# The second norm's products on 64-row halves of TensorE's array, in a kernel of four residual layers

## The chip, the cores and the metric

The kernel runs on one core of a Trainium2 chip. The metric is the device time of one execution in microseconds (us). The engines have these names in the profile: PE (TensorE, the matrix engine, with PEld for its weight loads), DVE (VectorE), ACT (ScalarE), POOL (GpSimd) and SP (SyncE, which here issues transfers). A product of the program in 32-bit floats shows in the trace as two weight loads and two matmul instructions.

## The reference

The input is 8 images of 64 channels, 128 x 128 pixels, in 32-bit floats. Four layers are applied, each as `x = x + L(_gn(x))`, where `_gn` is a group norm over 32 groups. L0 is a deformable convolution, L1 a 3x3 convolution, L3 a neighbour graph with a convolution and an attention factor. The change is in L2:

```python
def _s5_block(x, i, ...):                    # x: (images, 16384 positions, 64 channels)
    fx = _layer_norm(x, ln1_g[i], ln1_b[i])  # first norm, over the channels
    h = _s5_scan(fx, ...)                    # complex state-space scan, forward and backward
    x = jax.nn.gelu(h) + fx
    fx2 = _layer_norm(x, ln2_g[i], ln2_b[i]) # second norm, over the channels
    return fx2 @ ff_enc[i].T @ ff_dec[i].T + fx2
y_h = _s5_block(<positions row by row>, 0, ...)
y_v = _s5_block(<positions column by column>, 1, ...)
return einsum(concat(y_h, y_v), fusion_w) + fusion_b
```

## The kernel before

The images go through in four pairs; a tile has 2 x 64 = 128 partitions. Layer 0 (gathers issued by POOL) takes about the first 12,110 us. After it each pair passes the first norm, and then layer 2 in class `Scan`: direction d = 0 takes the positions row by row, d = 1 column by column. For each pair and direction `ahead` makes 16 steps g, each of 8 rows (or columns); that is 4 x 2 x 16 = 128 steps. Four successive positions are numbered 2h + e: in the scan's tiles e is the half of the 128 partitions, h and the image i are free dimensions, and 256 blocks of four positions are the innermost.

One step of `ahead` (the state of the backward scan was written to memory before) does these things, with the names of the tiles:

- `inputs` (L1236-1246): ACT scales the normed input into `fx`, and SP issues four loads `in<-fx`, which bring the two images' channels and the position parities into their partitions.
- `drive` (L1248-1262): PE makes `pv` from `in`, ACT copies it to `v` (one buffer), PE turns it into `pt`, DVE multiplies both by cosines and sines into `u` and `v`, and POOL adds them: `u`.
- `scan` (L1264-1277): DVE runs the recurrence, two instructions, into `z`; PE makes the start state `pn`.
- `rebuilt` (L1294-1308): for the backward state, loaded by SP into `zb` (one buffer), and for `z`: PE turns it into `zt`, POOL multiplies into `x` (L1305), DVE makes `xt`, POOL subtracts (L1307).
- `outputs` (L1310-1325): per half h, PE adds four products into `py`, ACT applies gelu, DVE adds the input: `h`.
- `mixed` (L1327-1345): the second norm. Its weights are folded ahead of time into two 128 x 128 matrices side by side, `outs[:, CEN : MIX + P]`: the centring (times 1/8) and the centring times `(ff_enc, ff_dec, ln2_g, fusion)`. Both are block-diagonal, one 64 x 64 block for each e. Per half h there are four products (m: which 128 of the 256 blocks; i: which image) with a 128 x 128 piece of `h` as weights and the 256 columns as moving operand, into `pc`, one PSUM bank for each m. ACT squares the centred 128 columns of each product into `qs` (named `sq` in the code) and copies the mixed ones to `ms`; DVE sums the squares over the channels to `var` (L1343). The reciprocal root of the variances, `rsqrt` (L112-122, tiles `ln_ve`, `ln_sh`, `ln_y`, `ln_t`), is a chain of 15 small DVE operations.
- `add` (L1347-1362): POOL multiplies `ms` by `ln_y` (L1353, two instructions), PE transposes back (`tp`, L1357), DVE adds to the running sum `room` (L1359) and, in d = 1, takes statistics for the next group norm (L1362).

Beside the steps of d = 0 the backward scan of d = 1 runs (`back`, through the generator `aside`), which doubles the `drive` and `scan` work of these steps; beside the last steps of d = 1 the end of layer 0 for the next pair runs. The PSUM tiles have three tags with two banks each (`x` for `pc`, `y` for `py`, `b` for `pv`, `pt` and `zt`) and two banks for small ones. The program lists the operations in the order of the code; which instruction stands where in each engine's queue is decided when it is built, by a scheduler, and an engine then takes them in that order.

```python
for m in range(2):
    pc = net.ps.tile([P, 2, 2 * P], F32, tag="x", name=f"pc{tag}_{h}{m}")
    for i in range(2):
        nc.tensor.matmul(pc[:, i], lhsT=hs[:, h, i, m * P : (m + 1) * P], rhs=self.outs[:, CEN : MIX + P], start=True, stop=True)
```

Of the kernel before, what the change touches and what calls it, by code (L numbers as in the profile page):

```python
# [9 lines left out]
F32 = mybir.dt.float32  # L10
I32 = mybir.dt.int32
AF = mybir.ActivationFunctionType
# [4 lines left out]
P = 128  # L17
C = 64
# [18 lines left out]
OUTM, INM, CEN, MIX = 0, T * P, T * P + 3 * P, T * P + 4 * P  # L37
# [1178 lines left out]
class Scan:  # L1216
# [110 lines left out]
    def mixed(self, g, hs):  # L1327

        nc, net, tag = self.nc, self.net, f"{self.p}_{self.d}_{g}"
        ms = [self.wp.tile([P, 2, 4, C], F32, tag=f"ms{h}", name=f"ms{tag}_{h}") for h in range(2)]
        var = net.small.tile([P, 16], F32, tag="var", name=f"var{tag}")
        for h in range(2):
            sq = self.wp.tile([P, 4, P], F32, tag="sq", name=f"qs{tag}_{h}", bufs=1)
            for m in range(2):
                pc = net.ps.tile([P, 2, 2 * P], F32, tag="x", name=f"pc{tag}_{h}{m}")
                for i in range(2):
                    nc.tensor.matmul(pc[:, i], lhsT=hs[:, h, i, m * P : (m + 1) * P], rhs=self.outs[:, CEN : MIX + P], start=True, stop=True)  # L1339
                nc.scalar.activation(sq[:, 2 * m : 2 * m + 2], pc[:, :, 0:P], AF.Square)  # L1340
                to = ms[h][:, :, 2 * m : 2 * m + 2].rearrange("p e i c -> p i e c")
                nc.scalar.copy(to, pc[:, :, P:].rearrange("p i (e c) -> p i e c", e=2))
            nc.vector.tensor_reduce(var[:, 8 * h : 8 * h + 8], sq.rearrange("p q (e c) -> p (q e) c", c=C), axis=mybir.AxisListType.X, op=ALU.add)  # L1343
            yield
        yield ms, net.rsqrt(net.small, var, 16, EPS, "ln16")
# [18 lines left out]
    def ahead(self, aside):  # L1364


        self.outs = self.wp.tile([P, NOUT], F32, tag="outs", name=f"outs{self.p}_{self.d}", bufs=1)
        self.nc.sync.dma_start(self.outs, self.net.out_tab[self.d])
        fxs, us, xs, late, z = {}, {}, None, None, None
        for g in range(-2, NG + 1):  # L1370
            if 0 <= g + 1 < NG:
                z = self.scan(0, g + 1, us.pop(g + 1), z, "z")
            hs = self.outputs(g, fxs.pop(g), xs) if 0 <= g < NG else None
            mixed = self.mixed(g, hs) if 0 <= g < NG else None
            if 0 <= g + 1 < NG:
                xs = [self.rebuilt(1, g + 1, None)]
            if mixed:
                next(mixed)
            if 0 <= g + 1 < NG:
                xs.append(self.rebuilt(0, g + 1, z))  # L1380
            if g + 2 < NG:
                fxs[g + 2] = self.inputs(0, g + 2, "in", "fx")
                us[g + 2] = self.drive(0, g + 2, fxs[g + 2])
            made = None
            if mixed:
                next(mixed)
                made = (g, *next(mixed))
            if late:
                self.add(*late)
            late = made  # L1390
            next(aside, None)
        for _ in aside:
            pass
# [48 lines left out]
```

## Time and profile before

| | |
|---|---|
| median of 10 runs | 16340.71 us (16333.48 to 16350.54) |
| profiled execution: its time, and its span from first to last instruction | 16354.39 us, 16352.6 us |
| mean granted clock of TensorE over the span | 0.823 |
| busy over the span: PE, DVE, POOL, ACT | 66%, 71%, 62%, 18% |
| layer 2's four stretches of 32 steps (first to last `py`) | 613.5, 611.4, 608.7, 596.4 us |
| a steady step of d = 0, of d = 1 | 21.4, 15.7 us |

The table's shares are means over stages with different limits: the gathers of layer 0 fill POOL for the first three quarters of the span, and say nothing of layer 2. So layer 2's own stretches are what to read. A step is counted from one group's first `py` to the next one's. In rows of the profile "idle before <-" names what ended the wait of an engine ahead of an instruction.

### The profile page before, as it was taken

To read this page: it belongs to the slowest core of one execution; us is meant where nothing else is said; L and a number is where in the kernel's file an instruction comes from. 1 tells how busy PE (TensorE), PEld (TensorE's weight loads), DVE (VectorE), ACT (ScalarE), POOL (GpSimd) and SP (SyncE) were. 2 spreads that over 40 slices of the span, in tenths; PEclk is the share of its full clock that TensorE was granted. 3 is DMA by queue.
4 is the path that set the end of the run, shared out by engine and by line. 5 is a ranking of instruction groups with operands and counts; after the bars stand their busy time and mean duration, and the time that the engine had idled before them with its cause. 6 is when DMAs were issued, how large, how long until landed. Compare 5 with 4: busy or idle time off the path is not lost. (4 is left out here: it accounts for less than half of the span.)

```text
span 16352.6 us, 119261 instructions
## 1 busy us (share of the span) xinstructions
PE 10871.1 (66%) x31736; PEld 4000.6 (24%) x31736; DVE 11662.1 (71%) x27948; ACT 2880.9 (18%) x4762; POOL 10194.1 (62%) x10484
## 2 busy tenths in 40 slices
PE   7864576367665635766556655643489888888896
PEld 2211121112211111211111111111135344344343
DVE  6777777777777777777777777777547558466566
ACT  1100111011000001110000000000144244243342
POOL 5777777777777777777777777777425135044142
PEclk9986798678887767988778877865699899999997
DMA  5444444345433334443333343333422433434223
GB/s 171 126 120 134 138 144 151 111 140 149 146 114 118 115 112 139 146 124 114 118 115 116 115 119 115 114 108 108 124 65 70 150 78 103 117 82 136 87 69 106
DMA packets 900135, 1933.41 MB, mean 118 GB/s; under 512 B 199932, under 2 KB 435844, under 8 KB 876420
## 3 DMA queue, kind: packets, MB, share of 16 engines
q0 software_dynamic: 442368, 1208.55, 25.5%
q1 hardware_dynamic: 382048, 679.50, 13.7%
q10 hardware_dynamic: 75044, 37.72, 1.1%
q8 instruction: 257, 4.21, 0.1%
q14 instruction: 418, 3.42, 0.1%
HBM read 1540.74 MB, written 208.10 MB: 107 GB/s over the span
## 5 line engine op out<-in xcount | busy, mean ns | idle before, releaser
L380 POOL DMA_INDIRECT g<-table,idx x9216 | 8721.2, 946 | 2823.9 <-issue 2631.9
L391 DVE TENSOR_TENSOR g<-g,corner_weights 128x256 f32<-128x256 f32 x9216 | 3768.7, 415 | 2722.6 <-DMA g<-table,idx 2685.4
L392 DVE TENSOR_REDUCE sm<-g 128x64 f32<-128x256 f32 x9216 | 5013.8, 579 | 8.9
L292 PE MATMUL po<-xe,wt 128*54 128x512 f32 (+3 forms) x8384 | 4300.9, 628 | 11.9 <-ACT ob L302 11.9
L398 PE MATMUL sp<-ident,sm 128*128 128x128 f32 x4096 | 1537.3, 380 | 4165.5 <-DVE sm L392 4151.1
L398 PEld LDWEIGHTS sp<-ident,sm 128*128 128x128 f32 x4096 | 630.2, 156 | 6732.4 <-DVE sm L392 5045.9
L403 ACT COPY s<-sp 128x512 f32<-128x512 f32 x1024 | 599.8, 586 | 8720.2 <-PE sp L398 8719.7
L292 PEld LDWEIGHTS po<-xe,wt 128*54 128x54 f32 x8384 | 902.8, 132 | 1343.0 <-issue 1062.4
L409 PE MATMUL yp<-s,wd 128*64 128x512 f32 (+1 forms) x2560 | 897.3, 711 | 25.6 <-ACT s L403 24.8
L891 POOL COPY l_yb<-ln_y 128x512 f32<-128x512 f32 x128 | 73.0, 615 | 1298.3 <-DVE ln_y L122 1298.3
L1261 POOL TENSOR_TENSOR u<-u,v 128x512 f32<-128x512 f32 x256 | 328.1, 1282 | 692.8 <-DVE v L1260 550.3
L607 PE MATMUL c<-room,l_w 128*64 128x508 f32 (+1 forms) x3072 | 741.8, 597 | 22.5 <-DMA room<-nx 14.0
L1353 POOL TENSOR_TENSOR ms<-ms,ln_y 128x512 f32<-128x512 f32 x256 | 274.2, 1092 | 638.8 <-DVE ln_y L122 608.4
L1243 ACT ACTIVATE fx<-room,ln_b,ln_g 128x512 f32<-128x512 f32 x512 | 639.1, 1292 | 172.4 <-DMA in<-fx 149.5
L1276 DVE TENSOR_TENSOR_SCAN z<-tabs,z,u 128x256 f32<-128x256 f32 x512 | 435.2, 876 | 214.7 <-POOL u L1261 186.0
L1254 PE MATMUL pv<-in,tabs 128*128 128x512 f32 x1024 | 509.2, 620 | 45.5 <-DVE u L1260 40.8
L1339 PE MATMUL pc<-outs,h 128*128 128x256 f32 x2048 | 501.8, 388 | 30.3 <-DVE h L1324 28.9
L1321 PE MATMUL py<-x,outs 128*128 128x512 f32 x1024 | 507.4, 599 | 7.8 <-POOL x L1307 7.3
L1321 PE MATMUL py<-in,outs 128*128 128x512 f32 x1024 | 505.6, 606 | 4.4 <-DMA outs<-out_tab 2.3
L1339 PEld LDWEIGHTS pc<-outs,h 128*128 128x128 f32 x2048 | 396.3, 195 | 207.4 <-issue 113.2
L1307 POOL TENSOR_TENSOR x<-x,xt 128x512 f32<-128x512 f32 x256 | 348.2, 1360 | 130.6 <-DVE xt L1306 130.1
L609 DVE TENSOR_TENSOR room<-room,c 128x512 f32<-128x512 f32 x128 | 87.9, 686 | 436.9 <-PE c L607 400.5
(416 smaller groups left out, 10175.8 us busy)
## 6 DMA issues: line engine op xcount, KB each, us to landing
g<-table,idx POOLq DMA_INDIRECT x9216, 2.7
in<-fx SPq DMA_DIRECT2D x1024, 128.0 KB
xe<-in_x_dram SPq DMA_DIRECT2D x56, 1408.0 KB
table<-q SPq DMA_DIRECT2D x256, 256.0 KB
y<-ys SPq DMA_DIRECT2D x128, 256.0 KB
room<-in_x_dram SPq DMA_DIRECT2D x64, 512.0 KB
yr<-y SPq DMA_DIRECT2D x64, 512.0 KB
room<-nx SPq DMA_DIRECT2D x256, 128.0 KB
```

The lines of the kernel that those rows point to most:

```text
L292: nc.tensor.matmul(po[:, r0:r1, c0:c1], lhsT=wt[:, t, :], rhs=xe[:, row + r0 : row + r1, c0 + dx : c1 + dx], start=n == 0, stop=n == len(u ...
L380: nc.gpsimd.indirect_dma_start(out=tq[:, k, :], out_offset=None, in_=flat[i], in_offset=bass.IndirectOffsetOnAxis(ap=idx[:, at : at + 1], ...
L391: nc.vector.tensor_mul(t[:, ks], t[:, ks], w)
L392: nc.vector.tensor_reduce(sm[:, ks], t[:, ks].rearrange("p k q c -> p k c q"), axis=mybir.AxisListType.X, op=ALU.add)
L398: nc.tensor.transpose(sp[:, j, :], sm[:, j * P : (j + 1) * P], self.ident)
L403: nc.scalar.copy(st[i][:, :, m * P : (m + 1) * P], sp)
L409: nc.tensor.matmul(yp[half[i], :], lhsT=wd[rows, j, :], rhs=src[rows, :], start=j == 0, stop=j == 4)
L607: nc.tensor.matmul(o, lhsT=lt, rhs=mv, start=k < 2, stop=k >= len(calls) - 2)
L1243: nc.scalar.activation(fx[:, e].rearrange("p h (o m) -> p h o m", m=self.INNER), src[:, e::2], AF.Identity, bias=w["ln1_b"], scale=w["ln1_g"])
L1254: nc.tensor.matmul(pv, lhsT=tabs[:, at : at + P], rhs=fx[:, :, h, :], start=h == 0, stop=h == 1)
L1321: nc.tensor.matmul(py, lhsT=lt, rhs=mv, start=n == 0, stop=n == len(calls) - 1)
L1339: nc.tensor.matmul(pc[:, i], lhsT=hs[:, h, i, m * P : (m + 1) * P], rhs=self.outs[:, CEN : MIX + P], start=True, stop=True)
```

## The change

`mixed` uses the block-diagonal form. Each product is made twice, once for each e: 64 partitions of `h` as weights, with the 64 rows of `outs` that belong to them, and of these the 64 + 64 columns of their own blocks (two strided runs). The two products of a pair go to different halves of the array's rows, and their results to two PSUM banks `pc[0]` and `pc[1]`, both of tag `x`; a bank now holds one e of all four (m, i), where it held both e of one m. In instructions of the trace, a step has 32 matmuls on 64 rows with 128 columns, where it had 16 on 128 rows with 256 columns. The number of ACT instructions and of their elements stays; a pair of them now waits for all products of its bank. The rest of the code is as it was, three lines further down; the built order of instructions on the engines differs in the steps of layer 2.

```diff
--- before.py
+++ after.py
@@ -1333,13 +1333,16 @@
         var = net.small.tile([P, 16], F32, tag="var", name=f"var{tag}")
         for h in range(2):
             sq = self.wp.tile([P, 4, P], F32, tag="sq", name=f"qs{tag}_{h}", bufs=1)
+            pc = [net.ps.tile([P, 4, 2, C], F32, tag="x", name=f"pc{tag}_{h}{e}") for e in range(2)]
             for m in range(2):
-                pc = net.ps.tile([P, 2, 2 * P], F32, tag="x", name=f"pc{tag}_{h}{m}")
                 for i in range(2):
-                    nc.tensor.matmul(pc[:, i], lhsT=hs[:, h, i, m * P : (m + 1) * P], rhs=self.outs[:, CEN : MIX + P], start=True, stop=True)
-                nc.scalar.activation(sq[:, 2 * m : 2 * m + 2], pc[:, :, 0:P], AF.Square)
-                to = ms[h][:, :, 2 * m : 2 * m + 2].rearrange("p e i c -> p i e c")
-                nc.scalar.copy(to, pc[:, :, P:].rearrange("p i (e c) -> p i e c", e=2))
+                    for e in range(2):
+                        rows = slice(e * C, (e + 1) * C)
+                        both = self.outs[rows, CEN : MIX + P].rearrange("p (k e c) -> p k e c", k=2, e=2)[:, :, e]
+                        nc.tensor.matmul(pc[e][:, 2 * m + i], lhsT=hs[rows, h, i, m * P : (m + 1) * P], rhs=both, start=True, stop=True)
+            for e in range(2):
+                nc.scalar.activation(sq[:, :, e * C : (e + 1) * C], pc[e][:, :, 0], AF.Square)
+                nc.scalar.copy(ms[h][:, e], pc[e][:, :, 1])
             nc.vector.tensor_reduce(var[:, 8 * h : 8 * h + 8], sq.rearrange("p q (e c) -> p (q e) c", c=C), axis=mybir.AxisListType.X, op=ALU.add)
             yield
         yield ms, net.rsqrt(net.small, var, 16, EPS, "ln16")
```

## The prediction

> **What bounds the kernel now.** I read the page first for the groups of the changed lines, then the windows view for two stretches of steady steps, then the timelines of PE, POOL, ACT and SP in one step of each kind. From the page (line, engine, operation, tiles, count, busy us and mean ns, idle time before them):
>
> ```profile
> L1261 POOL TENSOR_TENSOR u<-u,v 128x512 f32<-128x512 f32 x256 | 328.1, 1282 | 692.8 <-DVE v L1260 550.3
> L1353 POOL TENSOR_TENSOR ms<-ms,ln_y 128x512 f32<-128x512 f32 x256 | 274.2, 1092 | 638.8 <-DVE ln_y L122 608.4
> L1339 PE MATMUL pc<-outs,h 128*128 128x256 f32 x2048 | 501.8, 388 | 30.3 <-DVE h L1324 28.9
> L1339 PEld LDWEIGHTS pc<-outs,h 128*128 128x128 f32 x2048 | 396.3, 195 | 207.4 <-issue 113.2
> ```
>
> The changed products are 2048 instructions, 502 us of PE: 16 in each of 128 steps (four pairs, two directions, 16 groups). What a step is bound by differs by direction. The windows view, five steps along the rows, then six along the columns (length, then busy time of PE, PEld, DVE, ACT, POOL; clock):
>
> ```profile
> 12206.50:12313.50 107.00, 95.08 (x301) 50.77 (x300) 66.22 (x156) 49.67 (x91) 49.58 (x41) 1.00 0.30 74
> 12499.65:12593.85 94.20, 93.95 (x312) 53.58 (x311) 83.53 (x174) 41.48 (x84) 52.06 (x43) 1.00 0.21 52
> ```
>
> A row step takes 21.40 us, and PE is idle for 2.4 of them; a column step takes 15.70, and PE has no idle time. The clock is full in both, so the durations compare. PE in a column step (start, us, instruction, count):
>
> ```profile
> 12509.16 1.02 PE L1301 MATMUL zt<-zb,turn 128*128 128x512 f32 x2
> 12510.01 1.89 PE L1339 MATMUL pc<-outs,h 128*128 128x256 f32 x8
> 12511.74 1.02 PE L1301 MATMUL zt<-z,turn 128*128 128x512 f32 x2
> 12512.60 1.89 PE L1339 MATMUL pc<-outs,h 128*128 128x256 f32 x8
> 12514.33 0.60 PE L1357 MATMUL tp<-ident,ms 128*128 128x128 f32 x4
> 12514.76 0.28 PE L1269 MATMUL pn<-z,tabs 128*128 128x2 f32 x2
> ```
>
> From start to next start a block of eight takes 1.73 us, 0.216 a product of 256 columns; a product of 512 takes 0.43; four products of 128 take 0.43, 0.108 each with a full weight load each. In the row step PE's waits hang on other engines (its timeline, then ACT's and POOL's):
>
> ```profile
> 12217.88 1.98 PE L1254 MATMUL pv<-in,tabs 128*128 128x512 f32 x4 [0.89 <-DVE u L1260]
> 12219.70 1.02 PE L1321 MATMUL py<-x,outs 128*128 128x512 f32 x2
> 12222.19 1.12 PE L1257 MATMUL pt<-v,turn 128*128 128x512 f32 x2 [1.48 <-ACT v L1256]
> ```
>
> ```profile
> 12221.56 0.59 ACT L1256 COPY v<-pv 128x512 f32<-128x512 f32 x1 [6.05 <-POOL u L1261]
> ```
>
> ```profile
> 12218.25 2.05 POOL L1353 TENSOR_TENSOR ms<-ms,ln_y 128x512 f32<-128x512 f32 x2 [7.24 <-DVE ln_y L122]
> 12220.26 1.26 POOL L1261 TENSOR_TENSOR u<-u,v 128x512 f32<-128x512 f32 x1
> ```
>
> Read backwards: PE's pt waits for ACT's v, which waits for POOL's u (v has one buffer), which is queued behind the two ms multiplies, which wait for the end of the reciprocal root on DVE (ln_y), which starts from the second pc block. Both pc blocks and this chain are on the loop of the row step.
>
> **The block itself.** A half's eight instructions of 256 columns become sixteen of 128 columns on 64 rows, alternating between two half-row tiles. If the tiles run side by side, each does eight at 0.111 (a 128-column load from start to start): 0.89 us. Where neighbours on PE differ in tile shape, the trace shows 0.09 us more from start to start, and the first load, some 0.11, is exposed: 0.2 on entry, 0.2 on leaving (next to 512-wide products on the full array). Block 1.29, 0.44 less than 1.73. If the halves take turns: 16 x 0.111 + 0.4 = 2.18, 0.45 more. The nearest row for side by side is
>
> ```profile
> L409 PE MATMUL yp<-s,wd 64*64 64x512 f32 x512 | 138.7, 615 | 0.0
> ```
>
> 512 products of 512 columns in 138.7 us, 0.27 each against 0.43 for one alone: two quarter tiles did run at once. But these differ in rows and in columns; the change's tiles share all 128 columns, and no row of before shows that. I take side by side.
>
> The Trainium skill ("TensorE: Matmul & The Clock Gate", section "LDWEIGHTS (loading the stationary operand)") says that a load's time goes with columns and not with rows, so that half the rows save no load time: taken alone it speaks against the change and gives the 2.18 block. The page "TensorEngine Tiling (Array Packing)", section "Key Properties", says that tiles load and multiply in parallel, and gives the 1.29 block. It also says that a change of mode drains the engine, without a figure; the 0.09 us above is the trace's.
>
> ACT does as many evacuations of the same 256 elements, so it costs nothing itself; but one half now fills both x banks, and the second block must wait until all four evacuations of the first are done: 0.2 us after the block's end, four at a pitch of 0.28, 1.3 in all. PE does zt (0.86) and a change of shape (0.2) meanwhile: 0.3 uncovered where zt is ready, 1.3 where it isn't.
>
> **What moves (from the built order).** In the row steps POOL's u now stands ahead of the two ms multiplies, and on DVE the root's small operations are spread between the adds, the u and v multiplies and the scan; its last operation comes after the scan. In the column steps the DVE chain is spread likewise, and POOL has u, ms, ms, then the next x(zb). The work on SP is the same: zb, then four loads in<-fx.
>
> **Row step.** PE's work at start-to-start pitches: 32 instructions of 512 (16 py, 8 pv, 4 pt, 4 zt) x 0.43 = 13.7; eight tp 0.87; pn 0.3; blocks 2 x 1.73 = 3.46: 18.3 before, and 13.7 + 0.87 + 0.3 + 2 x 1.29 = 17.5 after. Waits: before 21.4 - 18.3 = 3.1, as start-to-start gaps. After, u no longer waits for the ms multiplies (2.05), so the wait for v falls from about 1.6 to what ACT needs after pv (0.2 + 0.6) with little work beside it: 0.5. The wait of pv for DVE's u stays at 1.0, the second block adds 0.3. 17.5 + 1.8 = 19.3, 2.1 less. Eleven steps of the sixteen have the steady form; the others, at the ends, hang on the filling and emptying, and I leave them: -23 us a pair. If the halves take turns, 19.3 + 1.8 = 21.1 less what the longer block covers of the waits: 20.8, -0.6 a step.
>
> **Column step.** Here PE's gain (0.9) could only be had if nothing else is late. The order makes a new loop. POOL and SP in a step of before:
>
> ```profile
> 12519.91 2.05 POOL L1353 TENSOR_TENSOR ms<-ms,ln_y 128x512 f32<-128x512 f32 x2 [4.25 <-DVE ln_y L122]
> 12522.76 1.26 POOL L1261 TENSOR_TENSOR u<-u,v 128x512 f32<-128x512 f32 x1 [0.80 <-DVE v L1260]
> 12524.31 1.39 POOL L1305 TENSOR_TENSOR x<-zb,tabs 128x512 f32<-128x512 f32 x1 [0.29 <-POOL u L1261]
> ```
>
> ```profile
> 12510.25 0.33 SPq L1299 DMA_DIRECT2D zb<-back  x1
> 12511.25 2.39 SPq L1245 DMA_DIRECT2D in<-fx  x4
> ```
>
> x(zb) frees the one zb buffer; SP's next zb load waits for it, and the in<-fx loads are queued behind that; PE's pv waits for the last of them. Before, ms was done before u, and POOL stood idle ahead of ms. After: PE pv 1.72, tp 0.43 and 0.2 to the next engine = 2.35; DVE add 1.12, u 0.6, bn 0.6, v 0.68 and a small operation, 3.2; POOL u 1.29; DVE scan pair and the root's end 1.7; POOL ms, ms, x(zb) 3.4; SP zb 0.33 and three further issues at 0.59, 2.1; the last in<-fx lands 2.4 after issue (median of this stretch, from issue to landing): 16.45 us, against PE's 15.7 - 0.9 = 14.8. So 16.5, 0.8 more, in some twelve steps: +10 a pair. With the landing at its 95th percentile (3.8) always, it would be 17.9. Without that loop DVE and POOL would end at about 15.0.
>
> **Sum.** -23 + 10, and 0 to +2 at the turn and the ends, where the second block's wait is bare: -11 a pair, -44 in all. The profiled execution (16354.4; 1.8 outside the span) is 13.7 over the median of the runs; the difference is applied to both: 16310 for a profile, 16297 for the median.
>
> **Rivals.** *Slower, halves take turns* (chance 0.16): row -0.6 x 11 = -7, column: the same loop with a longer block, 16.5 to 16.8, +0.8 to +1.1 x 12 = +10 to +13, edges, where blocks are bare, 0.9 a step x 10 = +9: about +13 a pair, +50. It decides once the sixteen products take over 1.8 us. For: no row has two tiles sharing columns, and the load rule. Against: L409's row. *The column loop is longer than I sum* (0.22): landings at 3.4 make 17.5, +1.8 x 12 = +22 a pair against -23: level, and with edges +2 to +4 a pair, about +10. For: loads meet each other in bursts; the loop has eight hand-overs. *The new loop isn't there* (0.1), because the loads get ahead: 15.0 in column steps, -8 instead of +10: -31 a pair, about -120. Against: the queue order on SP is fixed. *My sum* 0.52.
>
> **How the numbers follow.** A measurement of this kernel tells about 0.2%, 33 us, from no change. My sum's own range is -75 to -15 (from landing and hand-overs 0.4 a step either way: 12 x 0.4 x 4 = 19, and from the row step 0.3 x 11 x 4 = 13), of which about seven tenths pass -33. With the last rival: faster 0.47. Turns at +50 with the upper part of the long loop: slower 0.24. The rest, 0.29. The range takes in the long loop and about half of the turns: 16262 to 16388.
>
> **What would show it.** In the profile after, the pc blocks of sixteen should take 1.1 to 1.3 us to the next start (over 2 means turns); row steps 19.3, with POOL's u ahead of ms and pt's wait for v under 0.6; column steps 16.5, with PE idle for 1 to 1.7 us ahead of pv, released by in<-fx, and POOL's x(zb) directly after ms. It is wrong if column steps stay at 15.7 or less, if row steps don't get below 20.5, or if the second block waits for ACT by over 1 us in steady steps.

## The result, and the profile after

The changed kernel takes 16408.83 us (median of 8 runs, 16398.0 to 16420.2), the kernel before in the same comparison 16343.42 us (28 runs): a ratio of 1.0042, 95% interval 1.0033 to 1.0051. It is 65 us slower, where 44 us faster was forecast, and 21 us above the range.

The rows of the changed lines over the whole span, first from the groups by form, then from the page (busy us, mean ns, idle time before). PE is the matrix engine, POOL the one that multiplies `ms`:

```profile
L1342 PE MATMUL pc<-outs,h 64*128 64x128 f32 x4096 | 343.1, 290 | 30.2 <-DVE h L1324 24.2 <-ACT ms L1345 5.5
```

```profile
L1261 POOL TENSOR_TENSOR u<-u,v 128x512 f32<-128x512 f32 x256 | 346.3, 1353 | 1081.4 <-DVE v L1260 379.7
...
L1254 PE MATMUL pv<-in,tabs 128*128 128x512 f32 x1024 | 544.7, 655 | 164.2 <-DMA in<-fx 55.8
...
L1356 POOL TENSOR_TENSOR ms<-ms,ln_y 128x512 f32<-128x512 f32 x256 | 308.8, 1225 | 310.9 <-DVE ln_y L122 279.8
```

The products themselves became cheaper: 343 us of PE where it was 502. But PE now waits 164 us ahead of `pv` (45.5 before), and the largest share that the page puts down to one cause, 55.8 us, is the transfer `in<-fx`. POOL's `ms` takes 1.23 us where it took 1.09. Five row steps and six column steps in the windows view (length; busy time and count of PE, PEld, DVE, ACT, POOL; granted clock; DMA share; GB/s):

```profile
12200.46:12298.38 97.92, 92.62 (x384) 45.64 (x382) 76.08 (x156) 48.20 (x91) 51.73 (x40) 1.00 0.32 81
12469.42:12586.56 117.14, 100.16 (x411) 51.13 (x410) 80.57 (x174) 39.91 (x85) 54.88 (x43) 0.93 0.16 43
```

A row step takes 19.6 us here, 1.8 less than the 21.4 of before. A column step takes 19.5 in place of 15.7, PE is idle for 17.0 us of the six (2.8 a step, none before), and the granted clock, full before, is 0.93.

Added over the four pairs, in the traces: the first 15 steps of the row direction gave 73 us (1309 to 1236), the two steps at the turn cost 6, the next 11 column steps cost 109 (696 to 805), the last four, up to the end of the last group's `py`, 49: 32 for three steps and 17 for that group's own `py`. The three gaps between the stretches (last `py` to the next pair's first) gave 23, the time before layer 2 was 7 shorter, the rest gave 4. That makes the +57 between the two profiled spans, 16352.6 and 16409.2.

PE in one column step of after (12581 to 12592):

```profile
12581.44 1.02 PE L1301 MATMUL zt<-zb,turn 128*128 128x512 f32 x2
12582.39 1.16 PE L1342 MATMUL pc<-outs,h 64*128 64x128 f32 x16
12583.48 1.13 PE L1301 MATMUL zt<-z,turn 128*128 128x512 f32 x2
12584.54 1.45 PE L1342 MATMUL pc<-outs,h 64*128 64x128 f32 x16
...
12586.56 1.10 PE L1321 MATMUL py<-in,outs 128*128 128x512 f32 x2
12589.91 1.96 PE L1254 MATMUL pv<-in,tabs 128*128 128x512 f32 x4 [2.25 <-DVE ln_y L116]
```

The first block of sixteen takes 1.09 us to the next start, the second 1.38 (its products with e = 1 wait for ACT, which empties their bank last). `pv` waits 2.25 us. The row names DVE, but that DVE operation had no part in `pv`; what ended the wait was the landing of `in<-fx`, as POOL, SP and ACT of the same step show:

```profile
12577.35 1.27 POOL L1261 TENSOR_TENSOR u<-u,v 128x512 f32<-128x512 f32 x1 [7.71 <-DVE ln_y L122]
12580.34 2.37 POOL L1356 TENSOR_TENSOR ms<-ms,ln_y 128x512 f32<-128x512 f32 x2 [1.72 <-DVE ln_y L122]
12582.67 1.72 POOL L1305 TENSOR_TENSOR x<-zb,tabs 128x512 f32<-128x512 f32 x1
```

```profile
12584.41 0.33 SPq L1299 DMA_DIRECT2D zb<-back  x1
12584.85 2.38 SPq L1245 DMA_DIRECT2D in<-fx  x4
```

```profile
12589.88 2.43 ACT L1243 ACTIVATE fx<-room,ln_b,ln_g 128x512 f32<-128x512 f32 x2 [2.79 <-DMA in<-fx]
```

POOL ends x(zb) at 12584.39, SP issues the load of `zb` 0.02 us later, then the four loads `in<-fx` (to 12587.23). By the trace's record of the transfers the last of them lands at 12589.78. ACT, whose next `fx` waits for the same loads, starts at 12589.88, and `pv` at 12589.91. That is the loop that the prediction described. In the row step, u stands ahead of ms as the built order said, and pt's wait for v is 0.22 us in place of 1.48:

```profile
12228.76 1.13 PE L1257 MATMUL pt<-v,turn 128*128 128x512 f32 x2 [0.22 <-ACT v L1256]
```

### The profile page after: what moved, and what is told of

Its sections match the earlier page's. It is cut to its first block, busy times and chain, and to the rows that moved or that the text cites. A ratio compares the mean times of both kernels' runs of the same rounds, so it can differ in the third digit from the quotient of the medians.

```text
span 16409.2 us, 123363 instructions
## 1 busy us (share of the span) xinstructions
PE 10877.9 (66%) x33784; PEld 3942.4 (24%) x33784; DVE 11709.7 (71%) x27948; ACT 2850.7 (17%) x4762; POOL 10224.1 (62%) x10484
## 5 line engine op out<-in xcount | busy, mean ns | idle before, releaser
L1254 PE MATMUL pv<-in,tabs 128*128 128x512 f32 x1024 | 544.7, 655 | 164.2 <-DMA in<-fx 55.8
L1356 POOL TENSOR_TENSOR ms<-ms,ln_y 128x512 f32<-128x512 f32 x256 | 308.8, 1225 | 310.9 <-DVE ln_y L122 279.8
L1276 DVE TENSOR_TENSOR_SCAN z<-tabs,z,u 128x256 f32<-128x256 f32 x512 | 381.4, 760 | 88.1 <-POOL u L1261 59.1
L1324 DVE TENSOR_TENSOR h<-h,in 128x512 f32<-128x512 f32 x256 | 258.5, 1010 | 238.1 <-ACT h L1323 236.8
L1362 DVE TENSOR_TENSOR room<-room,tp 128x512 f32<-128x512 f32 x256 | 294.4, 1150 | 121.8 <-PE tp L1360 121.1
```

The source lines that it names most:

```text
L1254: nc.tensor.matmul(pv, lhsT=tabs[:, at : at + P], rhs=fx[:, :, h, :], start=h == 0, stop=h == 1)
L1276: nc.vector.tensor_tensor_scan(z[:, i, 1 : NB + 1], tabs[:, DEC : DEC + 1].to_broadcast([P, NB]), u[:, i, :], z[:, i, 0:1], ALU.mult, ALU.add)
```

## The experiments

Two theories remained to be told apart. The first: the products cost nothing; the order that the scheduler built around them opened a loop in the column direction (POOL's u, ms, ms, x(zb), then SP's zb and in<-fx, then pv, DVE, u). The rival: the half-row tiles, their changes of shape or their two banks, cost the column step its time. Edits below are against the changed kernel, or against the kernel before where said. "Behind" is an edge that fixes the order of two instructions on one engine without a wait for completion.

**e1: two buffers for zb in the column direction.**

```diff
-            zf = wp.tile([P, 2, NB], F32, tag="zb", ...)
+            if self.d and g % 2:
+                zf = wp.tile([P, 2, NB + 1], F32, tag="zbk", ...)[:, :, 0:NB]
+            else:
+                zf = wp.tile([P, 2, NB], F32, tag="zb", ...)
```

> The changed kernel, but in the column direction the loads of zb go alternately to two buffers (the second is the idle tile of the backward way), so that a zb load, and the four loads in<-fx queued behind it on SP, no longer wait for POOL's x(zb) of the step before. The built order on POOL, DVE and PE in a steady step is that of the changed kernel. Theory (the loop x(zb) -> zb load -> in<-fx loads -> pv -> ... -> ms -> x(zb) sets the column step): PE no longer waits for in<-fx, column steps fall from 18.0-20 to 15.0-15.5, the clock stays full, in all about 16245 us (11 steps x 3.5 x 4 pairs and the ends off 16409). Rival 1 (the half-row blocks themselves, with their changes of tile shape, cost PE the time): column steps stay above 18, 16409 +- 10. Rival 2 (the spread DVE chain with POOL behind it is a loop of its own): column steps 16.5-17.5, about 16330.

Measured: 16398.33 us, 1.0037 (1.0023 to 1.0051); column steps 18.7 on average, as in the changed kernel (18.6). The theory's forecast failed, and SP's waits show why the edit did not do what it was for (ten column steps):

```profile
SPq L1302 <- PE zt L1304: 123.8, 9, 14.7
SPq L1302 <- POOL x L1308: 21.0, 9, 2.5
```

The scheduler used the second buffer to put each zb load one step earlier in SP's queue (in ten of ten steps it is issued two groups ahead of its x(zb), in the changed kernel one), so that it still waits for an x(zb) of the step, and in<-fx still stands behind it. The wait moved with the buffer. So this run decides nothing between the theories.

**e2: half-row products only in the row direction; e3: only in the column direction** (`if self.d == 0` or `if self.d == 1` around the changed block, else the block of before).

> Half-row products only in the row direction (d = 0); the column direction as in the kernel before, in code and in built order. Theory: row steps 19.3-19.6 as in the changed kernel, column steps 15.7 as before; the row part gives its 73 us and the gaps between the stretches up to 20 more: 16250 to 16270. Rival (the two directions hang together, so that what the rows gain is lost in the columns): 16343 +- 15.

> Half-row products only in the column direction (d = 1). Theory: row steps 21.4, column steps 18-20 with PE waiting for in<-fx, about 16343 + 147 = 16490 less what the gaps give, 16470 to 16490. Rival (the changed row steps cause the slow column steps): column steps under 17, below 16390.

e2: 16262.36 us, 0.9953 (0.994 to 0.9967). Rows 19.4, columns 15.7. e3: 16457.84 us, 1.0075 (1.006 to 1.0091). Rows 21.4, columns 18.2, with the built order of after in the columns. So each direction nearly keeps its own step, whatever the other does (the changed kernel has 19.4 and 18.6). e3's total is 12 us below its forecast. In the whole, -78 and +117 make +39, against +65 for the changed kernel. The 26 us between are little more than the interval of one of these runs (22 us either way); in the profiles most of them lie in the gaps between the stretches, which gave 14 us in e2, 32 in e3 and only 23 in the changed kernel.

**e4: the same banks and order, full rows.**

```diff
-                        rows = slice(e * C, (e + 1) * C)
+                        rows = slice(0, P)
```

> The changed kernel with the same two banks, the same number of products and the same built order on all engines, but each product on all 128 rows (128 columns of the block-diagonal matrix, of which 64 rows are zero for it): only the use of half-row tiles is taken away. Theory: a block of sixteen takes 1.76 us in place of 1.09-1.4; the column step doesn't change, since its loop doesn't go through the blocks (18-20 us); row steps 20.0-20.5; in all 16430 to 16460. Rival (the half-row tiles slow the column step): column steps 15.7-16.5, in all 16300 to 16340.

Measured: 16415.0 us, 1.0048 (1.0032 to 1.0063), 15 below the forecast range; rows 20.3, columns 18.2, both as forecast. This is the control: 128-row products in the changed order (12508 to 12524) give

```profile
12515.59 1.95 PE L1342 MATMUL pc<-outs,h 128*128 128x128 f32 x16
12517.37 1.02 PE L1301 MATMUL zt<-z,turn 128*128 128x512 f32 x2
...
12523.82 1.96 PE L1254 MATMUL pv<-in,tabs 128*128 128x512 f32 x4 [1.87 <-DVE ln_y L116]
```

a block of 1.78 us in place of 1.09, and column steps nearly as slow as with half rows (44 of them 791 us, against 805 in after and 696 in before). So half-row tiles are not what costs the column step, and they do run side by side. The rival is out. In the rows they are worth 0.8 us a step (20.3 to 19.5 in the first pair).

**e5: zb behind in<-fx on SP, column direction.**

```diff
+                self.loaded = nc.sync.dma_start(out[...], fx[...])
...
+            if self.d:
+                with net.tc.issue_after(self.loaded.ins):
+                    nc.sync.dma_start(zf, net.back[self.d][g])
```

> The changed kernel with one edge of order on SP in the column direction: the load of zb stands behind the four loads in<-fx of the next group, not ahead of them. POOL, DVE and PE keep the changed kernel's built order. Theory (in<-fx waits on SP behind zb, which waits for x(zb)): that loop is cut, in<-fx lands 2.4 us after issue instead of 3.1 (zb no longer moves beside it), PE no longer idles ahead of pv and keeps the full clock; column steps 15.0-15.7, in all 16409 less 44 x 3.2 and part of the ends: 16240 to 16270. Rival (another loop through the DVE chain and POOL is nearly as long, as the unchanged step with two zb buffers could also mean): column steps 16.5-18.5, in all 16310 to 16400.

Measured: 16310.72 us (11 runs), 0.9984 (0.9975 to 0.9993); column steps 17.0 to 17.2. The order of the other engines is that of after, so this one edge is worth some 95 us (1.0042 to 0.9984): the loop through SP is shown. in<-fx now lands 2.37 us after issue (median), against 3.15 in after, where the 256 KB of zb move at the same time. But the step ends at 17.2 and not at 15.0 to 15.7, and the total some 40 us above the theory's range; in the windows view (six steps) PE still idles 1.6 us a step, at full clock:

```profile
12489.31:12591.64 102.33, 92.52 (x412) 47.26 (x410) 75.30 (x174) 39.56 (x85) 54.13 (x42) 1.00 0.19 49
```

So the rival of this run was right as well: there is a second loop, some 1.8 us shorter than the first.

**e6: the order of before in the column direction** (root ahead of the u multiply on DVE, ms ahead of u on POOL, by edges in `drive`, `mixed` and `add`, two more of which keep the v multiply behind the u multiply and the addition to `room` behind the root; half-row products in both directions).

```diff
+            if h and self.d and g + 2 in self.drives:
+                self.behind(self.drives[g + 2][1], mul.ins)    # POOL: u behind ms
...
+                self.root = self.nc.cur_bb.bb.instructions[-1]
+                if self.d and g + 2 in self.drives:
+                    self.behind(self.drives[g + 2][0], self.root)    # DVE: u multiply behind the root
```

> The changed kernel, with edges of order in the column direction that put the reciprocal root on DVE in one piece ahead of the u and v multiplies, and POOL's two ms multiplies ahead of u, as in the kernel before; half-row products in both directions. Theory (the order, not the products, costs the time): column steps 14.9-15.7, in all 16220 to 16262. Rival (the half-row products in two banks cost the column step even in the old order): column steps above 16.3, in all above 16290.

Measured: 16255.33 us, 0.9952 (0.9938 to 0.9965); column steps 16.0, 0.3 above the forecast and above the 15.7 of before. With the order put back and the changed products kept, it is some 150 us faster than the changed kernel. Together with e4 that settles the question of cause. The order isn't that of before in every place: POOL's is, but on DVE the u multiply still stands ahead of the second addition, and PE keeps the order of after. Whether that makes the 0.3 us was not tried. In the column direction, then, the cheaper products gained nothing in any run here.

**e7: the kernel before, one swap in the column direction: POOL's u ahead of ms.**

```diff
+            if self.d and g + 2 in self.totals:
+                net.tc.add_manual_dep(mul.ins, self.totals[g + 2].name, info, reason="order")
```

> The kernel before, products unchanged, with one swap in the column direction: on POOL u stands ahead of the two ms multiplies; DVE, PE and SP keep their order. Theory: the loop is there, without its term for the late end of the root (1.7 us): pv to add 2.4, DVE 3.1, POOL u 1.3, ms, ms and x(zb) 3.4-4.1, SP 2.2, landing 2.4-3.1 = 14.8-16.2 against PE's 15.7: column steps 15.7-16.5, in all 16340 to 16380. Rival (POOL's order by itself is what costs 3 us): column steps above 18, in all above 16440.

Measured: 16412.21 us, 1.0047 (1.0033 to 1.006). One swap on POOL, with the products of before, makes the kernel slower by 73 us. That this is near the +65 of the whole change is chance: here the rows gain nothing (21.4 us a step), and the column steps cost about half as much (eleven of each pair 751 us, against 805 in after and 696 in before). The column step is 17.0, and the total 32 us above the theory's range, between theory and rival; PE is hardly waiting for in<-fx (0.24 us ahead of `pv`). What holds it is the second loop, here with its length in the open (POOL, then DVE, then POOL of the next step):

```profile
12538.74 1.27 POOL L1261 TENSOR_TENSOR u<-u,v 128x512 f32<-128x512 f32 x1 [6.33 <-DVE v L1260]
12539.96 2.89 POOL L1355 TENSOR_TENSOR ms<-ms,ln_y 128x512 f32<-128x512 f32 x2
12542.81 1.65 POOL L1307 TENSOR_TENSOR x<-zb,tabs 128x512 f32<-128x512 f32 x1
12544.42 1.71 POOL L1307 TENSOR_TENSOR x<-z,tabs 128x512 f32<-128x512 f32 x1
12546.09 1.27 POOL L1309 TENSOR_TENSOR x<-x,xt 128x512 f32<-128x512 f32 x1
...
12555.78 1.27 POOL L1261 TENSOR_TENSOR u<-u,v 128x512 f32<-128x512 f32 x1 [6.33 <-DVE v L1260]
```

```profile
12547.40 0.69 DVE L1308 TENSOR_TENSOR xt<-zt,tabs 128x512 f32<-128x512 f32 x1 [1.20 <-POOL x L1309]
```

POOL works from u to the first subtraction without a pause, 12538.74 to 12547.36; DVE's xt waits for that (one buffer), and behind xt stand the sum of squares, an addition, the root (3.0), the second addition, u, a statistics operation and v; POOL's next u waits for v, at 12555.78. 8.62 on POOL and 8.42 on DVE are 17.04 us. In the kernel before, POOL does ms (12519.91 to 12521.96, shown in the prediction) while DVE does the second addition, u and v, so that ms is not a link of this loop, and PE's 15.7 us set the step:

```profile
12519.68 1.21 DVE L1359 TENSOR_TENSOR room<-room,tp 128x512 f32<-128x512 f32 x1
12520.81 0.68 DVE L1260 TENSOR_TENSOR u<-pv,tabs 128x512 f32<-128x512 f32 x1
...
12522.01 0.67 DVE L1260 TENSOR_TENSOR v<-pt,tabs 128x512 f32<-128x512 f32 x1
```

**e8: e6 and e5 together.**

> The changed kernel with both repairs of order in the column direction: root and ms ahead of u (as in e6), and the load of zb behind the four loads in<-fx on SP (as in e5). If what e6's column step (16.0) has above PE's own 14.8 is still the wait of pv for in<-fx, it goes to 15.0-15.4 and the whole to 16215-16235. Rival (the loop through DVE and POOL, without SP, holds it): 15.8-16.2, in all 16245 to 16265.

Measured: 16265.76 us, 0.9954 (0.9941 to 0.9968); column steps 16.0. The forecast of 15.0 to 15.4 failed; the step is the rival's, the total just above its range. SP's waits name a third release for in<-fx, DVE's addition that is the last reader of the `in` buffer (ten steps):

```profile
SPq L1245 <- DVE h L1331: 122.4, 10, 13.8
```

Whether that alone holds the step at 16.0 was not tried.

**e9: the kernel before, one swap in the row direction: POOL's u ahead of ms** (the edit of e7 with `not self.d`).

> The kernel before, products unchanged, with one swap in the row direction: on POOL the u of the forward way stands ahead of the two ms multiplies; all else in the order of before. It tells how much of the row step's 21.4 to 19.4 is order: the prediction's term for it was 1.1 us a step (the wait for v from 1.6 to 0.5). Theory: row steps 20.2-20.6, in all 16340 less 48 x 1.0 = 16285 to 16305. Rival (it is the shorter blocks that give the row step its time): row steps above 21, in all above 16325.

Measured: 16285.38 us, 0.9963 (0.995 to 0.9977); row steps 20.0, a little under the forecast, and the column steps as before. The wait of pt for v, 1.48 us before, is gone (PE, 12254 to 12258):

```profile
12254.35 1.02 PE L1323 MATMUL py<-x,outs 128*128 128x512 f32 x2
12255.39 1.13 PE L1257 MATMUL pt<-v,turn 128*128 128x512 f32 x2
```

Of the 2.0 us that the change takes off the row step, 1.4 are order, too, and can be had without the change. The fastest versions are e6, e2 and e8 (0.995), equal within their intervals; e9 (0.996) and e5 (0.998) beat both kernels as well.

## Why the prediction was wrong

*The block* held, with a cheaper price: 1.09 us where 1.29 was summed, 1.38 with the wait for ACT in it, and the tiles run side by side (e4).

*The row step* held: 19.3 forecast, 19.4 the median, u ahead of ms, pt's wait under 0.6. The order's share was larger than booked, 1.4 us (e9) where the wait for v was to give 1.1. The sum over the rows was too large, 73 us where 4 x 23 = 92 were booked, since the mean of the steady steps is 19.5 to 19.8 (single steps of 20 to 23), not 19.3.

*The column step* is what failed, and in it the terms of the new loop; the loop itself is there (e5). Forecast 16.45, measured 18.99 from `pv` to `pv` as the mean of 41 steps:

| term | forecast | after |
|---|---|---|
| pv start to DVE's add | 2.35 | 3.23 (2.43 to 4.64) |
| DVE: add to POOL's u | 3.2 | 3.16 |
| POOL u, then scan and end of root | 3.0 | 2.99 |
| POOL ms, ms, x(zb) | 3.4 | 4.08 |
| SP: zb to the last in<-fx issue | 2.1 | 2.41 |
| last in<-fx issue to pv | 2.4 | 3.11 |

Three prices were taken from the steady step of before, in which these operations have other neighbours. Each is different in the place that the change moves it to:

- **PE's clock** (+0.9). A price at full clock was used for a step in which PE was to wait by the same sum. One step's stretch before `pv` (which starts at 12570.65) and two behind it in the windows view, columns as above:

```profile
12557.80:12570.65 12.85, 10.01 (x54) 5.29 (x53) 9.47 (x19) 3.69 (x12) 9.05 (x7) 1.00 0.25 63
12570.65:12573.20 2.55, 2.55 (x5) 0.97 (x6) 1.21 (x7) 2.41 (x2) 0.00 (x0) 0.72 0.00 0
12573.20:12576.30 3.10, 3.10 (x10) 1.83 (x9) 2.09 (x4) 0.58 (x1) 0.00 (x0) 0.68 0.00 0
```

  After PE's wait the mean granted clock of these stretches is 0.7 (half the clock for 3.4 us), and the products between `pv` and `tp`, which are on the loop, take up to 2.2 us longer: the step is then 20 instead of 18. A wait on PE that is long enough lengthens itself. The 1 to 1.7 us of wait that the prediction expected would not have done it by these runs: in the changed kernel's steady column steps no wait under 2.5 us was followed by a slow period. It was the other two terms that made the wait long enough.
- **POOL** (+0.7). ms took 1.05 each where DVE beside it did the addition to `room` and the u multiply, each with an input in PSUM; in after it takes 1.2 and x(zb) 1.72 (1.39 before), beside DVE's `h` additions, whose two inputs are in SBUF. In e5 ms takes 1.5, x(zb) 1.27: the price goes with what runs beside it.
- **The landing and SP** (+1.0 together). In before, 1.5 us (median) lay between the zb issue and the first in<-fx; in after they are issued together (0.44), and in<-fx lands in 3.15 in place of 2.37. e5 gives the 2.37 back.

The prediction had this case as a rival, "the column loop is longer than I sum", but priced it by a longer landing alone, at about +10; the other two terms, the clock above all, made the loop longer than that. Twelve column steps of each pair cost 127 us (759 to 886) where the sum had 4 x 10 = 40.

*The turn and the ends* were booked at 0 to +2 a pair and cost 38 us in all: 6 at the turn, 15 in the last two steps, 17 in the last group's `py` (39 to 56). The 17 are gone in e5 (36), which differs in zb's place on SP alone; the rest was not taken apart.

*The floor of 15.0 for DVE and POOL* in the column step was wrong for the same reason: 17.0 to 17.2 (e5, e7), of which the POOL stretch in e7 is 8.6 where its six operations at 1.03 to 1.27 would be 7.1. The prediction gave no working for the 15.0. The rival "the new loop isn't there" (-120) therefore could not have come out in this order: cutting the first loop leaves 17.2.

*The gaps between the stretches*, not in the sum at all, gave 23 us.

## What to carry to other kernels

When an edit shifts a scheduled order, price each operation of a new loop by its new neighbours: a POOL operation beside other DVE work, a load that is issued together with another, a PE stretch after a wait. A faster product on an engine that is waiting buys nothing, and most of the gain here was to be had by one swap of order (e9, 0.9963 against 0.9952 for the best) with no change to the products. Before an order is accepted, look for what now stands in front of the last reader of a single buffer, and compare versions that differ in that edge alone.

## What the runs showed of the hardware

Two half-row tiles that share all 128 columns do load and multiply at the same time: sixteen products of 64 rows take 1.09 us from start to next start, sixteen of 128 rows 1.78, at full clock.

In eleven column steps of the first pair, seven of the nine waits of PE of 2.6 to 3.4 us ahead of `pv` were followed by 3.4 us at half clock; the two of 2.2 us were not, and in the column steps of e5 and e7, where PE waits less, the clock stayed full. The Trainium skill ("TensorE: Matmul & The Clock Gate", section "What's actually happening") gives half the clock after at least one idle window of about 3.4 us; the length of the slow period agrees with that, but here shorter waits were enough.

POOL's and DVE's operations stretch each other: in e7's column steps ms takes 1.46 us and DVE's scan beside it 1.50, where the scan takes 0.75 in after and ms 1.05 in before, with other neighbours. The Trainium skill ("GPSIMD Engine Reference", section "Specifications") says that the two share their SBUF interfaces, with contention when a DVE instruction has two SBUF inputs, as the scan and the h addition have; the rows fit that, and no run here took it apart.
